# Last image's feed-forward: normalisation as subtraction and product of eight columns, second bias and residual in parts of four columns, and an order of its own

## The chip, the cores and the metric

The kernel runs on one core of one Trainium2 chip. The time is device microseconds (us) of one execution; lower is better. Five engines work side by side, each through a queue of its own in a fixed order: TensorE (PE, its weight loads listed as PEld), VectorE (DVE), ScalarE (ACT), GpSimd (POOL) and SyncE (SP, which only issues transfers here).

## What is computed

The input holds 8 images of 128 × 128 positions with 96 channels, in fp32. One layer is computed. Its first half normalises over the channels, projects to 192 channels, transforms each image with a two-dimensional Fourier transform, multiplies by filters that depend on the image, transforms back, projects to 96 channels and adds the input. Its second half is the feed-forward part, which the change is about:

```python
def _ln_t(v, eps=1e-5):
    m = jnp.mean(v, axis=-1, keepdims=True)
    s = jnp.var(v, axis=-1, keepdims=True)
    return (v - m) / jnp.sqrt(s + eps)
...
def _qlinear(x, W, b):
    y = q_acc(jnp.einsum('bsk,nk->bsn', q_mul(x), q_mul(W)))
    return q_acc(y + q_mul(b))
h = jax.nn.relu(_qlinear(x, W1, b1))
y = _qlinear(h, W2, b2)
...
t = t + _L0_ffn_ref(_ln_t(t), L0_ffn_W1, L0_ffn_b1, L0_ffn_W2, L0_ffn_b2)
```

`q_mul` rounds to a float with 5 exponent and 2 mantissa bits (fp8e5 in the kernel), `q_acc` to one with 5 and 10 (f16). W1 is 384 × 96, W2 is 96 × 384.

## The kernel before

Each image goes through three streams. Stream "a" (function `before`) normalises, projects, squares and makes the first transform, and stores the result in DRAM. Stream "s" (`spectrum`) does the second transform, the filters and the way back, with many small matmuls on quarters of the PE array, and stores to V in DRAM; its last PE step is L1241. Stream "c" (`after`) does the last inverse transform (L1337), the residual and the feed-forward part.

Stream "c" works in 8 blocks of 16 image columns (`WB`); a column is a slice of 96 channels for the 128 rows, one row per partition. A block has 4 quarters of 4 columns (`QW`), so an image has 32 units. For a block: SP loads t, the image's input, and vin from V (L1331, L1332); PE multiplies a quarter of vin (L1337), DVE adds t (L1343) and takes statistics column by column (L793, `measure`). `rstd` then gives the scale and shift of the 16 columns: `variance` on GpSimd (L803 to L807), `root` on ACT (L812), `inverse` on DVE (L816), `rest` on GpSimd (L597 to L600, and L824 to L826 for the shift). `quantise` makes each column t·r + m in fp8e5, on ACT (L1361) or on DVE (L1359); every eighth column is on DVE, and for the last image, number 7, every second.

For a unit, PE transposes 4 columns (`turn`, L1366), a cast brings them to SBUF (`turned`, L1380 on ACT; for image 7 L1378 on DVE), PE makes three products of 128 hidden channels (`first`, L1384), ACT casts each to f16 (L1391), DVE adds the first bias (`biased`, L1395), ACT takes the positive part (L1404; for image 7 the last third on DVE, L1402), PE multiplies with W2 (`second`, L1411) and ACT casts to f16 (`put`, L1422). After the 4 units of a block, GpSimd adds the second bias to the whole block (L1426) and then the block to t (L1429), and SP stores it (L1432). Most tiles have two buffers, t has five.

A planner, `in_order`, fixes the order of each queue before the program is built. Every step is an `Op` with the steps that it needs; the planner plays the five engines with the durations in `COST`, and picks, among the steps that can begin within `WAIT` of the earliest, the one with the lowest place plus `PATIENCE` times its delay (and, on PE, `TURN` for a change between quarter and full array). The place is the window of image and stream in `WINDOWS` plus an offset by kind in `OFFSETS`. `SHARED` names the DVE steps that the planner keeps apart from GpSimd's. Each engine then keeps that order. Streams of different images overlap, so ahead of the last image's end stream "c" of one image lies beside "a" and "s" of later ones. The feed-forward part of image 7 needs the whole stream "s" of image 7 (`load_v` waits for every `store_v`).

`WARM` lists PE steps ahead of which some filler matmuls are issued (`keep_warm`, L587); their output is not used.

Of the kernel before, what the change touches and what calls it, by code (L numbers as in the profile page):

```python
# [68 lines left out]
    "a": ((-1014.7, 224.2), (1155.2, 782.6), (913.1, 640.2), (700.4, 97.1), (81, 727.1), (986.1, 683.8), (1759.7, 398.2), (2087.9, 538.4)),  # L69
    "s": ((159.4, 351.5), (85.6, 1024.7), (720.2, 346.4), (408.4, 331.2), (-141.4, 469.9), (-95.4, 205.3), (797.8, 257), (1809.8, 30.5)),  # L70
    "c": ((1028.7, 511.2), (1109.6, 188.3), (1290.9, 349.7), (1829.7, 439.1), (2176.6, 456.9), (2490.5, 149.5), (2420.5, 484.7), (2163.8, 1143.1)),
}
OFFSETS = {
    "a_context": -69.32,
    "a_fold": 73.44,
    "a_inverse": -262.16,
    "a_load_r": 18.09,
    "a_load_x": 271.95,
    "a_load_xT": -31.56,
    "a_measure": 23.91,  # L80
    "a_project": 117.85,
    "a_put": 26.98,
    "a_rate_e": 26.43,
    "a_rate_n": 275.68,
    "a_rate_p0": -178.47,
    "a_rate_p1": 125.73,
    "a_rate_p2": -434.33,
    "a_rate_v0": -18.7,
    "a_rate_v1": 37.77,
    "a_rate_v2": 27.67,  # L90
    "a_rate_v3": 53.52,
    "a_rectify": -24.16,
    "a_rest": 88.21,
    "a_root": -155.19,
    "a_scale": 83.17,
    "a_square": 92.51,
    "a_store_r": 7.65,
    "a_store_y": -218.91,
    "a_transform": -124.2,
    "a_variance": -11.06,  # L100
    "c_accumulated": -194.42,
    "c_add_up": -37.31,
    "c_bias": -232.6,
    "c_biased": -34.16,
    "c_first": -3.46,
    "c_hidden": -99.06,
    "c_hidden_2": 18.08,
    "c_hidden_v": 120.54,
    "c_inverse": -69.89,
    "c_last": -164.57,  # L110
    "c_load_v": -0.91,
    "c_measure": 206.09,
    "c_put8": 55.17,
    "c_quantise": 161.11,
    "c_quantise_v": 272.29,
    "c_residual": -76.16,
    "c_rest": -195.99,
    "c_root": 122.09,
    "c_second": -129.32,
    "c_store": 584.16,  # L120
    "c_turn8": -377.8,
    "c_turned8": 104.13,
    "c_turned8_v": -71.45,
    "c_variance": -123.83,
    "s_alone_t": 236.02,
    "s_alone_x": 109.24,
    "s_alone_z": 223.71,
    "s_along_w": -28.38,
    "s_combine": -31.52,
    "s_copy_sr": 140.45,  # L130
    "s_filters_of": 27.98,
    "s_invert": 0.86,
    "s_inverted": -111.88,
    "s_load_t": 225.43,
    "s_load_y": 199.13,
    "s_make": 124.58,
    "s_mix": 88.61,
    "s_mix_low": -10.96,
    "s_mixed": -366.14,
    "s_store_v": 136.77,  # L140
    "s_times": -505.74,
    "s_turn_back": 28.39,
    "s_weigh": -53.57,
}
WAIT, PATIENCE, TURN = (0, 0, 0, 0.27, 0.89), (85, 74.3, 16.6, 0.273, 8.9), 454.49
# [5 lines left out]
    ('c', 1): {('second', 12): 4, ('second', 18): 4},  # L151
    ('s', 2): {('along_w', 7): 4},
    ('a', 3): {('project', 6, 0): 3},
    ('c', 5): {('second', 21): 20, ('second', 29): 10},
# [47 lines left out]
    "s_alone_x": (POOL, 1.01, 0),  # L202
    "c_last": (PE, 0.845, 0),
    "c_residual": (DVE, 0.552, 0),
    "c_measure": (DVE, 0.738, 0),
    "c_quantise": (ACT, 0.48, 0),
    "c_quantise_v": (DVE, 0.323, 0),
    "c_turn8": (PE, 0.386, 0),
    "c_turned8": (ACT, 0.59, 0),
    "c_turned8_v": (DVE, 0.68, 0),  # L210
    "c_hidden_v": (DVE, 0.6, 0),
    "c_hidden_2": (ACT, 1.06, 0),
    "c_first": (PE, 0.381, 0),
# [1343 lines left out]
```

## Time and profile before

| | us |
|---|---|
| median of 3 runs | 2740.46 (2726.29 to 2744.11) |
| profiled execution, its own time | 2741.53 |
| its span, from first to last instruction | 2739.4 |

| stage (us) | PE busy | DVE busy | ACT busy | POOL busy | PE clock |
|---|---|---|---|---|---|
| 0 to 200 | 168.68 | 117.96 | 78.80 | 58.86 | 0.87 |
| 200 to 600 | 382.47 | 328.66 | 237.49 | 208.62 | 0.99 |
| whole span | 2517.3 | 2280.6 | 2143.5 | 1691.3 | 0.966 |

Busy times are those in which an engine executes at least one instruction; the clock is the share of full speed that was granted to TensorE. A group of the profile, such as "L1395 DVE TENSOR_TENSOR y<-y,b1q", is one line of the kernel on one engine: output and inputs by the program's names, sizes as partitions × elements, the count, the busy time, the mean duration of one in ns, and then the idle time of the engine just ahead of them with what ended it ("<-ACT y L1391"). In a list of waits, "ACT h L1404 <- DVE y L1395: 14.4, 11, 2.8" reads: ACT was idle ahead of L1404 until L1395 on DVE had ended, for 14.4 us in 11 cases, the longest 2.8. In the order in time, a row has its start, its duration, engine, line and names.

### The profile page before, as it was taken

Reading aid. Unit: us, or ns where it says so; the run is one execution under the profiler, and the core shown is the slowest. Engines: PE = TensorE matmul, PEld = TensorE weight load, DVE = VectorE, ACT = ScalarE, POOL = GpSimd, SP = SyncE. Lnnn points to the kernel's source line nnn. Section 1 sums busy time; section 2 is a strip of 40 time slices with the busy share of each in tenths; the row PEclk is TensorE's granted clock in tenths of the full one; section 3 lists DMA queues with packets and bytes.
Section 4 is the critical chain, followed back from the end, with each engine's and each line's share of the span. In section 5 each row is a group of like instructions: output and inputs, shape, how many; then the busy total and the mean of one; then the engine's idle time right before and its main releaser. Section 6 shows DMA issues by size and latency. Waiting matters only on the chain.

```text
span 2739.4 us, 92861 instructions
## 1 busy us (share of the span) xinstructions
PE 2517.3 (92%) x37514; PEld 1803.0 (66%) x37514; DVE 2280.6 (83%) x5485; ACT 2143.5 (78%) x4332; POOL 1691.3 (62%) x2535
## 2 busy tenths in 40 slices
PE   7899999999899999899999999999999998999887
PEld 4557777767667776666776776766667665666444
DVE  5568697888898888978888988888979988889786
ACT  2356666649889798887998788988989888988866
POOL 3235454546576657756777576857766676788444
PEclk8899999999999999999999999999999999999889
DMA  8789899998867987587768988786768666575341
GB/s 227 243 262 302 255 279 291 285 272 276 260 192 244 291 258 204 186 259 240 231 198 258 289 257 260 224 243 199 234 190 250 192 201 187 153 230 157 107 137 46
DMA packets 506110, 621.22 MB, mean 227 GB/s; under 512 B 165197, under 2 KB 440038, under 8 KB 505658
## 3 DMA queue, kind: packets, MB, share of 16 engines
q1 hardware_dynamic: 417618, 464.28, 57.7%
q10 hardware_dynamic: 88064, 151.02, 15.5%
q8 instruction: 295, 4.83, 0.8%
q14 instruction: 133, 1.09, 0.1%
HBM read 407.03 MB, written 208.16 MB: 225 GB/s over the span
## 4 chain that ended last, share of the span: by engine, by line
PE 42%; ACT 17%; DVE 11%; issue 6%; DMA 4%; POOL 3%; ACTq 0%; SPq 0%; POOLq 0%; DVEq 0%
PE px L881 7%; PE py L910 6%; PE pv L1200 5%; ACT y L1391 4%; PE pf L1119 4%; PE pz L1104 4%; PE pg L1241 4%; PE pk L1337 4%; ACT h L1404 3%; ACT z L1361 3%; PE ph L1384 3%; PE po L1411 2%; DMA vin<-Vd 2%; DVE y L1395 2%; DVE t L1148 1%
## 5 line engine op out<-in xcount | busy, mean ns | idle before, releaser
L881 PE MATMUL px<-W1S,zT 97*128 97x240 f32 x2048 | 505.0, 381 | 10.6 <-DVE yst L922 5.5
L881 PEld LDWEIGHTS px<-W1S,zT 97*128 97x128 f32 x2048 | 393.1, 196 | 123.6 <-PE warm L587 10.4
L1089 POOL TENSOR_TENSOR tw<-tb,r 128x384 f32<-128x384 f32 (+1 forms) x264 | 292.1, 1106 | 259.2 <-PE pf L1119 127.6
L910 PE MATMUL py<-X,F 128*128 128x384 f32 x1024 | 435.3, 515 | 17.0 <-DVE t L1343 3.1
L1391 ACT CAST y<-ph 128x512 f16<-128x512 f32 x768 | 417.1, 604 | 25.6 <-PE ph L1384 21.6
L1404 ACT ACTIVATE h<-y 128x1536 fp8e5<-128x1536 f16 (+1 forms) x256 | 371.1, 1450 | 29.2 <-DVE y L1395 26.3
L892 ACT ACTIVATE rl<-px 128x480 f32<-128x480 f32 x512 | 292.7, 579 | 127.5 <-PE px L881 94.1
L1361 ACT ACTIVATE z<-t,ln_m,ln_r 128x96 fp8e5<-128x96 f32 x848 | 361.3, 475 | 9.1 <-POOL ln_m L826 5.6
L1395 DVE TENSOR_TENSOR y<-y,b1q 128x1536 f16<-128x1536 f16 x256 | 321.5, 1256 | 54.2 <-ACT y L1391 52.8
L906 POOL TENSOR_TENSOR sacc<-sacc,rl 128x192 f32<-128x192 f32 x248 | 175.1, 706 | 289.4 <-ACT rl L892 277.3
L1200 PE MATMUL pv<-w2C,xf 64*64 64x96 f32 x9264 | 315.6, 246 | 28.5 <-issue 25.4
L922 DVE TENSOR_TENSOR yst<-py,yb 128x384 f32<-128x384 f32 x512 | 261.7, 546 | 74.0 <-ACT rl L892 24.2
L1200 PEld LDWEIGHTS pv<-w2C,xf 64*64 64x64 f32 x9264 | 273.2, 134 | 62.7 <-issue 45.7
L1142 DVE TENSOR_TENSOR d<-pz,sr 128x390 f32<-128x390 f32 x512 | 265.2, 554 | 42.1 <-ACT sr L1135 41.7
L1148 DVE TENSOR_TENSOR t<-d,pf 128x780 f32<-128x780 f32 x256 | 245.3, 958 | 53.2 <-PE pf L1119 33.2
L1162 POOL TENSOR_TENSOR xf<-t 128x390 f32<-128x390 f32 x256 | 234.5, 916 | 66.6 <-DVE t L1148 57.6
L1119 PE MATMUL pf<-RW,tw 64*128 64x130 f32 x3120 | 252.4, 292 | 20.8 <-DVE t L1153 11.1
L1104 PE MATMUL pz<-F,yt 64*64 64x65 f32 x12480 | 250.0, 223 | 18.6 <-issue 13.2
L1384 PE MATMUL ph<-zT,W1q 96*128 96x512 fp8e5 x768 | 242.1, 387 | 23.3 <-ACT y L1391 6.5
L1426 POOL TENSOR_TENSOR o<-o,b2q 128x1536 f16<-128x1536 f16 x64 | 200.5, 3132 | 94.1 <-ACT o L1422 93.5
L1104 PEld LDWEIGHTS pz<-F,yt 64*64 64x64 f32 x12480 | 217.3, 136 | 61.4 <-issue 26.9
L1119 PEld LDWEIGHTS pf<-RW,tw 64*128 64x128 f32 x3120 | 201.3, 189 | 82.8 <-issue 30.2
(132 smaller groups left out, 5129.7 us busy)
## 6 DMA issues: line engine op xcount, KB each, us to landing
Yd<-yst ACTq DMA_DIRECT2D x256, 384.0 KB
yt<-Yd SPq DMA_DIRECT2D x248, 384.0 KB
xb<-in_xw SPq DMA_DIRECT2D x64, 768.0 KB
zT<-in_xT SPq DMA_DIRECT2D x128, 384.0 KB
rB<-Rd SPq DMA_DIRECT2D x128, 384.0 KB
tb<-T SPq DMA_DIRECT2D x256, 192.0 KB
Vd<-gst ACTq DMA_DIRECT2D x128, 384.0 KB
t<-in_x SPq DMA_DIRECT2D x64, 768.0 KB
```

What stands on the lines that cost most here:

```text
L881: nc.tensor.matmul(px[:, i * (MED + SCTX) : (i + 1) * (MED + SCTX)], lhsT=zTs[(b * NU // 2 + u // 2) % NZT][:, QW * (u % 2) + i0 + i, :], ...
L892: nc.scalar.activation(kept["rl", u][:, i0 : i0 + 2, :].rearrange("h w m -> h (w m)"), kept.pop(("px", u, i0)), AF.Relu)
L910: nc.tensor.matmul(py, lhsT=F1, rhs=kept["X", u][:, i0 : i0 + 2, :].rearrange("h w m -> h (w m)"), start=True, stop=True)
L1089: nc.gpsimd.tensor_tensor(tw[p, :].rearrange("p (q k m) -> p k q m", q=3, k=2), tb[p, :].rearrange(order, k=2, q=3), rates[b][p, :].rearra ...
L1104: nc.tensor.matmul(halves[i][64 * k : 64 * k + 64, c * L : (c + 1) * L], lhsT=kept["yt", g][rows, 2 * cs + k, 64 * q : 64 * q + 64], rhs=F ...
L1119: nc.tensor.matmul(pf[:, s, q * 2 * L : (q + 1) * 2 * L], lhsT=tw[p, 128 * q : 128 * q + 128], rhs=RW[p, :], start=True, stop=True,)
L1200: nc.tensor.matmul(kept["pv", p, r][half, i * C : (i + 1) * C], lhsT=kept["xf", g][rows, k, q, half], rhs=(w2N if k == 1 and h == 1 else w ...
L1361: nc.scalar.activation(z, t, AF.Identity, bias=m, scale=r, saturate=False)
L1384: nc.tensor.matmul(kept["ph", u, n], lhsT=W1q[:, n * 128 : (n + 1) * 128], rhs=kept["zT", u], start=True, stop=True)
L1391: nc.scalar.copy(kept["y", u][:, n, :], kept.pop(("ph", u, n)))
L1395: nc.vector.tensor_tensor(y, y, b1q, ALU.add)
L1404: nc.scalar.activation(h, y, AF.Relu, saturate=False)
```

## The change

For image 7 alone:

- The normalisation is done for 8 columns at once, in two steps. `centre` on GpSimd subtracts the mean from 8 columns of t and writes into vin; `norm` on DVE multiplies them with r into fp8e5. `rstd` makes the mean (and not the shift) right after the variance. The 16 column-wise instructions of a block become 2 and 2.
- The transposed cast is on ACT (`turned8`), as for the other images; L1378 goes.
- The second bias and the sum with t are made unit by unit (`bias_part`, `add_part`). The last block is stored in four parts (`store_part`); the others are stored whole.
- `load_v` waits for the `norm` of two blocks ahead as well, since vin is written and read later than before.

In addition, `OFFSETS` may hold a value of its own for a kind in image 7 (ending `_8`) and in stream "a" of image 0 (ending `_1`; all of these equal those without the ending). `WINDOWS`, `OFFSETS`, `WAIT`, `PATIENCE`, `TURN` and `WARM` have new values for all images; only a few are shown. `SHARED` stays as it is. The filler matmuls are 510 instead of 472, of which 301 instead of 249 belong to stream "c" of image 7.

```diff
--- before.py
+++ after.py
@@ -66,95 +66,140 @@
 WINDOWS = {
...
-    "c": ((1028.7, 511.2), (1109.6, 188.3), (1290.9, 349.7), (1829.7, 439.1), (2176.6, 456.9), (2490.5, 149.5), (2420.5, 484.7), (2163.8, 1143.1)),
...
+    "c": ((1077.8, 438.5), (962.8, 173.4), (1098.5, 307), (1684.2, 504.4), (1984, 366.6), (2465, 69), (2244, 686.2), (2737, 1205.9)),
 }
 OFFSETS = {
...
+    "c_add_part_8": -199.88,
...
+    "c_bias_part_8": 1548.65,
...
+    "c_centre_8": 49.3,
...
+    "c_norm_8": -808.2,
...
+    "c_residual_8": -2157.99,
...
-WAIT, PATIENCE, TURN = (0, 0, 0, 0.27, 0.89), (85, 74.3, 16.6, 0.273, 8.9), 454.49
+WAIT, PATIENCE, TURN = (0, 0, 0, 0.25, 0.91), (3.5, 1.09, 73.9, 2.99, 3.82), 45.03
...
@@ -203,11 +248,12 @@
     "c_last": (PE, 0.845, 0),
     "c_residual": (DVE, 0.552, 0),
     "c_measure": (DVE, 0.738, 0),
+    "c_centre": (POOL, 1.65, 0),
+    "c_norm": (DVE, 0.95, 0),
     "c_quantise": (ACT, 0.48, 0),
     "c_quantise_v": (DVE, 0.323, 0),
     "c_turn8": (PE, 0.386, 0),
     "c_turned8": (ACT, 0.59, 0),
-    "c_turned8_v": (DVE, 0.68, 0),
     "c_hidden_v": (DVE, 0.6, 0),
     "c_hidden_2": (ACT, 1.06, 0),
     "c_first": (PE, 0.381, 0),
@@ -247,6 +293,9 @@
     "s_load_y": (SP, 0.9, 1.25),
     "s_load_t": (SP, 0.65, 0.576),
     "c_load_v": (SP, 2.1, 4.736),
+    "c_bias_part": (POOL, 0.84, 0),
+    "c_add_part": (POOL, 0.82, 0),
+    "c_store_part": (SP, 0.4, 0.48),
     "s_store_v": (ACT, 0.375, 1),
     "c_store": (SP, 0.4, 1.92),
     "_load_raw": (SP, 1.2, 1),
@@ -377,13 +426,19 @@
     return (stream[0] if stream else "") + "_" + name
 
 
+def group_of(op):
+
+    kind = kind_of(op)
+    return kind + "_1" if op.key[0] == ("a", 0) else kind + "_8" if op.key[0] == ("c", B - 1) else kind
+
+
 def place_of(op):
 
     if op.key[0] is None:
         return op.time
     x, b = op.key[0]
     start, length = WINDOWS[x][b]
-    return start + op.time * length + OFFSETS.get(kind_of(op), 0.0)
+    return start + op.time * length + OFFSETS.get(group_of(op), 0.0)
 
 
 SAME = {"alone_z": "make", "alone_t": "times", "alone_x": "turn_back"}
@@ -792,7 +847,7 @@
         for i in range(q * QW, (q + 1) * QW):
             nc.vector.bn_stats(st[:, i, :], xin[:, i, :])
 
-    def rstd(time, step, pool, key, kept, eps, one, users, mean=False):
+    def rstd(time, step, pool, key, kept, eps, one, users, mean=""):
 
 
         def variance(key):
@@ -806,6 +861,10 @@
             nc.gpsimd.tensor_scalar(d, d, C / 4, C * eps, ALU.mult, ALU.add)
             nc.gpsimd.tensor_tensor(v, v, d, ALU.add)
             kept["vd", key] = v, d
+            if mean == "centre":
+                m = kept["m", key] = pools[pool].tile([128, WB], F32, name="ln_m", tag="ln_m")
+                nc.gpsimd.tensor_tensor(m, st[:, :, 1], st[:, :, 4], ALU.add)
+                nc.gpsimd.tensor_scalar(m, m, 0.5, None, ALU.mult)
 
         def root(key):
             r = pools[pool].tile([128, WB], F32, name="ln_r", tag="ln_r")
@@ -819,14 +878,15 @@
             v, d = kept.pop(("vd", key))
             r, st = kept["r", key], kept.pop(("st", key))
             newton(r, v, d, C)
-            if mean:
+            if mean == "shift":
                 m = pools[pool].tile([128, WB], F32, name="ln_m", tag="ln_m")
                 nc.gpsimd.tensor_tensor(m, st[:, :, 1], st[:, :, 4], ALU.add)
                 nc.gpsimd.tensor_tensor(m, m, r, ALU.mult)
                 nc.gpsimd.tensor_scalar(m, m, -0.5, None, ALU.mult)
                 kept["m", key] = m
 
-        at(time, variance, key, after=[one("measure", key, q) for q in range(NQ)] + [one("rest", key - 2)])
+        free = [one("centre", key - 2, h) for h in range(2)] if mean == "centre" else []
+        at(time, variance, key, after=[one("measure", key, q) for q in range(NQ)] + [one("rest", key - 2)] + free)
         at(time + step, root, key, after=[one("variance", key)] + users)
         at(time + 1.5 * step, inverse, key, after=[one("root", key)])
         at(time + 2 * step, rest, key, after=[one("inverse", key)])
@@ -1319,7 +1379,7 @@
     def after(b, t0, P):
 
         stream[0] = "c", b
-        blocks = ("measure", "variance", "rest", "load_v", "store", "add_up", "turn8", "residual", "last", "quantise", "quantise_v")
+        blocks = ("measure", "variance", "rest", "load_v", "store", "add_up", "turn8", "residual", "last", "quantise", "quantise_v", "norm", "centre")
         one = named("c", b, {None: NU, **dict.fromkeys(blocks, NWB)})
         kept = {}
 
@@ -1348,7 +1408,19 @@
             add_stats(kept["st", blk], kept["t", blk], q)
 
         def quantiser(i):
-            return "quantise_v" if i % 8 == 7 or b == B - 1 and i % 2 == 1 else "quantise"
+            return "norm" if b == B - 1 else "quantise_v" if i % 8 == 7 else "quantise"
+
+        def centre(blk, h):
+            w = slice(h * HB, (h + 1) * HB)
+            m = kept["m", blk][:, w].unsqueeze(2).to_broadcast([128, HB, C])
+            nc.gpsimd.tensor_tensor(kept["vin", blk][:, w, :], kept["t", blk][:, w, :], m, ALU.subtract)
+
+        def norm(blk, h):
+            if ("z8", blk) not in kept:
+                kept["z8", blk] = pools["c"].tile([128, WB, C], F8, name="z8", tag="z8")
+            w = slice(h * HB, (h + 1) * HB)
+            r = kept["r", blk][:, w].unsqueeze(2).to_broadcast([128, HB, C])
+            nc.vector.tensor_tensor(kept["z8", blk][:, w, :], kept["vin", blk][:, w, :], r, ALU.mult, saturate=False)
 
         def quantise(blk, i):
             if ("z8", blk) not in kept:
@@ -1374,10 +1446,7 @@
         def turned(u):
             kept["zT", u] = pools["c"].tile([C, QW * 128], F8, name="zT8", tag="zT8")
             pz = kept.pop(("pz",) + divmod(u, NQ))[:C, :]
-            if b == B - 1:
-                nc.vector.tensor_copy(kept["zT", u], pz, saturate=False)
-            else:
-                nc.scalar.activation(kept["zT", u], pz, AF.Copy, saturate=False)
+            nc.scalar.activation(kept["zT", u], pz, AF.Copy, saturate=False)
 
         def first(u, n):
             kept["ph", u, n] = bank("ph")
@@ -1428,6 +1497,18 @@
         def add_up(blk):
             nc.gpsimd.tensor_tensor(kept["t", blk], kept["t", blk], kept["o", blk], ALU.add)
 
+        def bias_part(blk, q):
+            o = kept["o", blk][:, q * QW : (q + 1) * QW, :]
+            nc.gpsimd.tensor_tensor(o, o, b2q.unsqueeze(1).to_broadcast([128, QW, C]), ALU.add)
+
+        def add_part(blk, q):
+            w = slice(q * QW, (q + 1) * QW)
+            nc.gpsimd.tensor_tensor(kept["t", blk][:, w, :], kept["t", blk][:, w, :], kept["o", blk][:, w, :], ALU.add)
+
+        def store_part(blk, q):
+            w0 = blk * WB + q * QW
+            nc.sync.dma_start(out=out[b, :, w0 : w0 + QW, :], in_=kept["t", blk][:, q * QW : (q + 1) * QW, :])
+
         def store(blk):
             nc.sync.dma_start(out=out[b, :, blk * WB : (blk + 1) * WB, :], in_=kept.pop(("t", blk)))
 
@@ -1438,25 +1519,31 @@
             t = t0 + u * P
             blk, q = divmod(u, NQ)
             if q == 0:
-                after = [one("last", blk - 2, n) for n in range(NQ)] + [one("store", blk - 5)]
+                after = [one("last", blk - 2, n) for n in range(NQ)] + [one("norm", blk - 2, h) for h in range(2)] + [one("store", blk - 5)]
                 after += [(("s", b), "store_v", p) for p in range(NP)]
                 if b == 0 and blk < 2:
                     after += [(None, "next_pool")]
                 at(t - 0.004, load_v, blk, after=after)
-                users = [one(k, blk - 2, i) for i in range(WB) for k in ("quantise", "quantise_v")]
-                rstd(t, 0.3 * P, "c", blk, kept, 1e-5, one, users, mean=True)
+                users = [one(k, blk - 2, i) for i in range(WB) for k in ("quantise", "quantise_v", "norm")]
+                rstd(t, 0.3 * P, "c", blk, kept, 1e-5, one, users, mean="centre" if b == B - 1 else "shift")
             at(t, last, blk, q, after=[one("load_v", blk)], banks=1, until=[one("residual", blk, q)])
             at(t + 0.0003, residual, blk, q, after=[one("last", blk, q)])
             at(t, measure, blk, q, after=[one("residual", blk, q), one("rest", blk - 2)])
-            for i in range(QW):
+            if b == B - 1 and q % 2:
+                h = q // 2
+                after = [one("residual", blk, n) for n in (q - 1, q)] + [one("last", blk, n) for n in (q - 1, q)]
+                at(t, centre, blk, h, after=[one("variance", blk)] + after)
+                after = [one("rest", blk), one("centre", blk, h)] + [one("turn8", blk - 2, n) for n in range(NQ)]
+                at(t, norm, blk, h, after=after)
+            for i in range(QW if b < B - 1 else 0):
                 at(
                     t + 0.2 * i * P, quantise, blk, q * QW + i,
                     name=quantiser(q * QW + i),
                     after=[one("rest", blk), one("residual", blk, q)] + [one("turn8", blk - 2, n) for n in range(NQ)],
                 )
-            after = [one(quantiser(q * QW + i), blk, q * QW + i) for i in range(QW)]
+            after = [one("norm", blk, q // 2)] if b == B - 1 else [one(quantiser(q * QW + i), blk, q * QW + i) for i in range(QW)]
             after += [one("first", u - 2, n) for n in range(NHC)]
-            turned8 = "turned8_v" if b == B - 1 else "turned8"
+            turned8 = "turned8"
             at(t, turn, blk, q, name="turn8", after=after, banks=1, until=[one(turned8, u)])
             after = [one("turn8", blk, q)] + [one("first", u - 2, n) for n in range(NHC)]
             at(t + 0.0003, turned, u, name=turned8, after=after)
@@ -1471,13 +1558,21 @@
             for name, *part in hiddens:
                 at(t, hidden, u, *part, name=name, after=[one("biased", u), one("second", u - 2)])
             at(
-                t, second, u, after=[one(name, u, *part) for name, *part in hiddens] + [one("add_up", blk - 2)],
+                t, second, u, after=[one(name, u, *part) for name, *part in hiddens] + [one("add_up", blk - 2)] + [one("add_part", blk - 2, n) for n in range(NQ)],
                 banks=1, until=[one("put8", blk, q)],
             )
-            at(t + 0.0003, put, blk, q, name="put8", after=[one("second", u), one("add_up", blk - 2)])
-            if q == NQ - 1:
+            at(t + 0.0003, put, blk, q, name="put8", after=[one("second", u), one("add_up", blk - 2)] + [one("add_part", blk - 2, n) for n in range(NQ)])
+            if b == B - 1:
+                at(t, bias_part, blk, q, after=[one("put8", blk, q)])
+                zs = [one("centre", blk, q // 2)]
+                at(t, add_part, blk, q, after=[one("bias_part", blk, q)] + zs)
+                if blk == NWB - 1:
+                    at(t, store_part, blk, q, after=[one("add_part", blk, q)])
+                elif q == NQ - 1:
+                    at(t, store, blk, after=[one("add_part", blk, n) for n in range(NQ)])
+            elif q == NQ - 1:
                 at(t, bias, blk, after=[one("put8", blk, n) for n in range(NQ)])
-                zs = [one(quantiser(i), blk, i) for i in range(WB)]
+                zs = [one(k, blk, i) for i in range(WB) for k in ("quantise", "quantise_v", "centre")]
                 at(t, add_up, blk, after=[one("bias", blk)] + zs)
                 at(t, store, blk, after=[one("add_up", blk)])
 
```

## The prediction

> **What bounds the kernel now.** I read the 40 slices first, then sums by stage, then groups, waits and order in time for the last stage. TensorE leads: 2517.3 of 2739.4 us busy, 92% of the span. The sums by stage (us; each engine's busy time with its count; granted clock, DMA share, GB/s) show that this doesn't hold to the end:
>
> ```profile
> 600.00:2534.00 1934.00, 1802.16 (x30604) 1325.22 (x30604) 1682.41 (x3854) 1680.90 (x3460) 1332.74 (x1863) 0.98 0.75 228
> 2534.00:2739.40 205.40, 163.98 (x1071) 87.79 (x1069) 151.53 (x336) 146.32 (x284) 91.04 (x118) 0.90 0.31 97
> ```
>
> The columns are PE, its weight loads, DVE, ACT, POOL. Up to 2534 us PE is busy 93% of the time. From 2534 us on, when the last spectral product (L1241) is done, only the feed-forward of images 6 and 7 is left. I call this the tail. No engine fills it: PE 80%, DVE 74%, ACT 71%, POOL 44%, and the groups of the tail show that 70.6 us of PE's 164 are filler (L587):
>
> ```profile
> L587 PE MATMUL warm<-zeros 128*64 128x512 bf16 x279 | 70.6, 400 | 1.0 <-DVE zT L1378 0.9
> ...
> L1395 DVE TENSOR_TENSOR y<-y,b1q 128x1536 f16<-128x1536 f16 x38 | 47.4, 1251 | 22.8 <-ACT y L1391 22.4
> ...
> L1359 DVE TENSOR_SCALAR z<-t,ln_r,ln_m 128x96 fp8e5<-128x96 f32 x66 | 35.0, 565 | 1.1 <-POOL ln_m L826 1.1
> ...
> L1361 ACT ACTIVATE z<-t,ln_m,ln_r 128x96 fp8e5<-128x96 f32 x79 | 31.9, 478 | 2.1 <-POOL ln_m L826 2.1
> ...
> L1378 DVE CAST zT<-pz 96x512 fp8e5<-96x512 f32 x32 | 21.8, 682 | 10.2 <-PE pz L1366 9.7
> ```
>
> The mean of z on DVE, 565 ns, is far above its median over the run (322 ns), and y's 1251 above its 959. The order in time says why; two such places, DVE and then POOL:
>
> ```profile
> 2674.85 2.96 DVE L1359 TENSOR_SCALAR z<-t,ln_r,ln_m 128x96 fp8e5<-128x96 f32 x1
> ...
> 2678.60 3.09 DVE L1359 TENSOR_SCALAR z<-t,ln_r,ln_m 128x96 fp8e5<-128x96 f32 x1
> ...
> 2674.66 3.08 POOL L1426 TENSOR_TENSOR o<-o,b2q 128x1536 f16<-128x1536 f16 x1 [16.33 <-ACT o L1422]
> 2677.82 3.80 POOL L1429 TENSOR_TENSOR t<-t,o 128x1536 f32<-128x1536 f32 x1
> ```
>
> A 0.3 us instruction lasts as long as the block-wide GpSimd addition beside it. Against their shortest forms I count 32 us of such excess on y, z and h in the tail, 13 of 14 cases between 1.0 and 2.9 us. Last, what ACT and POOL wait for in the tail:
>
> ```profile
> POOL o L1426 <- ACT o L1422: 70.2, 8, 16.3
> ...
> ACT h L1404 <- DVE y L1395: 14.4, 11, 2.8
> ...
> ACT o L1422 <- PE po L1411: 10.1, 10, 2.8
> ACT ln_r L812 <- POOL ln_v L807: 9.9, 3, 4.7
> ...
> ACT y L1391 <- PE ph L1384: 8.5, 8, 3.3
> ```
>
> So the tail is a loop PE, ACT, DVE, PE in which each waits for the others, with GpSimd cutting in. ACT idles 59 us of 205: the 43 above, 4 on smaller rows, 10.5 at the end, after its last instruction.
>
> **What the Trainium skill says.** "SBUF — State Buffer", section "Who interferes with whom": DVE in a two-port mode, or with two inputs in SBUF, and GpSimd exclude each other for a whole instruction. The trace agrees (2.96 beside 3.08 us). The new product reads two SBUF tiles (vin, ln_r), so by this page it too is blocked by GpSimd, though the planner's set SHARED leaves it out. "VectorE: DVE Perf Modes", section "Why `tensor_tensor` can't do 2×_2P or 4×": fp32 stays at one element per cycle, so 768 columns at 0.96 GHz are 0.80 us at least (an estimate from the page). The nearest row, L1148 with 780 columns and one PSUM input, has a median of 957 ns.
>
> **The change part by part** (image 7: 8 blocks of 16 columns, 32 units of 4).
>
> 1. *Normalisation.* 128 instructions go: 64 on DVE (0.24 us each in a row: 15 us, without stalls) and 64 on ACT (0.36 us each in a row: 23). In come 16 products on DVE at 0.80 to 0.96, I take 0.9: 14 us; and 16 subtractions on GpSimd. GpSimd's two-input additions cost 0.888 us at 390 columns and 3.1 at 1536, on a line 1.62 at 768: 26 us. The mean's statistics change by one instruction of 0.25 per block: nothing. The 32 transposed casts move from DVE (0.60 in a row, 19 us off) to ACT (0.49, 16 us on). Net: DVE −20, ACT −7, GpSimd +26.
> 2. *Bias and residual in parts.* 16 instructions become 64 at 0.88: 50 us become 56. The longest hold of the shared port falls from 3.1 us to 0.9, or 1.6 for a subtraction. y (42 in the new tail), h (32) and the products (16) then meet shorter waits, oftener: 90 of them at 0.6 (chance that GpSimd is busy: about 120 of 185 us) × 0.45 (half a hold) are 24 us, against 32. More important is what waits behind: ACT's 14.4 us for y drop to 5, I estimate, since y can no longer be held up by 3 us; the square root's 9.9 us behind whole-block additions to 5. Both estimates could be zero gains.
> 3. *The end.* The last bias and sum, 3.08 + 3.09 us, become 0.88 + 0.88: −4.4. The last store is a quarter as large; from the end of the sum at 2735.2 to the span's end are 4.2 us, of which 0 to 3 may go, I take 1.5. Together −6, on the path for certain.
> 4. *Waits added.* In the built order GpSimd does variance, mean, both subtractions, and only then the rest of the rstd: 3.2 us are put ahead of it, and product and transpose wait for it; square root and reciprocal cover about 1.5. Eight times 1.7 are 14 us if nothing hides it; blocks run in pairs, with units of the earlier pair between, so I take +3. Behind a subtraction that waits for its residual stand the parts of bias and sum of earlier blocks, for which only stores and the L1422 casts two blocks on wait: nothing. The buffer vin is freed by the product instead of the last L1337, so loads of V start some us later; the load at 2639.2 feeds products up to 2649.6, and there are two buffers: taken as nothing, at most 8 × 2 us. SP issues the same loads and three more small stores; loads now stand in pairs behind pairs of stores, and the same cover hides it.
> 5. *Order.* The planner's constants and windows are new for all images, so every queue is reshuffled. The built orders nevertheless look alike: 566 and 572 switches between quarter-array and full matmuls on PE, the same sequence of stages. After the last L1241 stand 41 units instead of 39: two units of image 6 move into the tail. They cost ACT there about 3.7 us each (three casts 1.43, h 1.37, zT 0.49, o 0.37) and save about as much ahead: nothing. Filler matmuls ahead of the last L1241 fall from 176 to 134; 42 × 0.25 are 10 us of PE where PE bounds, half of it in true gaps: −5. Otherwise the reshuffle ahead of 2534 us is unknown: PE idles 150 us between 200 and 2534, and a tenth either way is ±15, taken as 0.
>
> The sum, on ACT as the engine that carries the tail (about 146 us of work before and after: −7 and the +7 of the two units): idle for y −9, for the square root −5, the end −6, idle behind PE −2 (PE waited for z and zT on DVE), work −7, subtraction ahead of rstd +3, filler −5: −31. Rounding against myself by 2 for PE, which carries more filler (see below): −29 from the profiled 2741.5, **2712 us**. That execution lies 1 us above the median of the runs, 2740.46, and within their spread of 18.
>
> **Rivals.**
>
> *A. The filler becomes the work.* The new tail has 376 filler matmuls instead of 296. PE busy 164 + 80 × 0.25 + 4.5 for two units are 188 us, at the mean clock of 0.90; with about 10 us of unavoidable idle the tail is 198 instead of 205 + 7: −14, less what a full clock gives back. With the −5 ahead: 2722. For it: filler was on the chain with 3.6 us at 2614. Against it: filler stands where PE waits.
>
> *B. The shared port decides, and it ends slower.* GpSimd in the tail: 56 + 26 + statistics 20 + three whole pairs of image 6 19 = 121 us; y 42 × 0.88, h 32 × 0.33, products 14, together 62. If they exclude each other fully, 183 us, against 84 + 60 = 144 before, which filled 70% of 205. If again only 75% can be filled, the tail is 244 instead of 212: +32, less 6 and 5: 2763, 23 above the median; the worst additions under 4 would pass 1%. It decides once usable filling stays below about 84%. Against it: the small GpSimd instructions overlap their start with a DVE hold, and shorter holds pack better.
>
> *C. The reshuffle ahead dominates.* ±15 us there on top of any case; for 2712 it gives 2697 to 2727.
>
> *D. Nothing changes in the tail*, because latency through buffers of two sets the pace, not work: only the end's −6 and −5 remain: 2730.
>
> **How the numbers follow.** Forecast with its reshuffle, somewhat better or worse: 0.58; A 0.12; D 0.12; B 0.18. A measurement of this kernel tells about 1% from no change: below 2713 or above 2768. Of the forecast's share some five sevenths fall below 2713, since both unknown stalls and packing could give more than I booked; from the others 0.08. That gives faster 0.50. B puts 0.15 past 2768, with its added waits and C's loss; a little more comes from C alone: slower 0.17. Same: 0.33. The range leaves one in ten out on either side: low 2675 (forecast; the rest of the gaps for y and the root gone, −10; stalls at the port halved, −12; C −15), high 2755 (most of B).
>
> **What would show it.** Right: DVE busy in the tail near 125 us, ACT near 146, no y, z or h above 2.7 us except beside image 6's additions; the last GpSimd addition near 0.9 us; 35 or so idle us on ACT. Products well over 1 us mean the port blocks them. A tail over 205 us with GpSimd and port-bound DVE work near 183 is B; PE over 95% with filler is A; a tail shorter by 25 with the same end is C. The forecast is wrong if the tail shrinks by less than 10 us, or if the stretch ahead moves by more than 15.

## The result, and the profile after

| | before | changed |
|---|---|---|
| median of 15 runs each (us) | 2738.36 (2723.9 to 2748.74) | 2716.31 (2709.7 to 2732.18) |
| span of the profiled execution (us) | 2739.4 | 2712.0 |
| granted TensorE clock in it | 0.966 | 0.976 |

The ratio is 0.9929, interval 0.9908 to 0.995. That is 19 us of 2738 (14 to 25), where 29 were forecast; the two medians lie 22 us apart.

The tail begins when the last spectral product has ended: at 2526.6 us before and at 2514.6 us after. I cut both profiles there (the prediction took 2534 for it before, 7 us late). The columns of the sums by stage are again PE, its weight loads, DVE, ACT and POOL, then clock, DMA share and GB/s. Before:

```profile
2526.60:2739.40 212.80, 170.50 (x1111) 90.94 (x1110) 156.98 (x339) 153.72 (x300) 98.03 (x125) 0.90 0.32 101
```

After:

```profile
600.00:2514.60 1914.60, 1780.27 (x30647) 1317.04 (x30648) 1676.13 (x3861) 1661.10 (x3430) 1333.03 (x1849) 0.98 0.75 230
2514.60:2712.00 197.40, 177.37 (x1240) 95.93 (x1238) 143.13 (x268) 155.01 (x286) 155.30 (x193) 0.98 0.36 115
```

The tail has become 15.4 us shorter. ACT works as long in it as before (153.7 and 155.0 us), so its idle time carries all of the difference: 59.1 us before, 42.4 after. GpSimd has gone from 98 to 155 us, and DVE has lost only 14. The other 12 us of the two spans lie ahead of the tail. The experiments show below that this point moves by more than that between executions, so I don't count them as an effect.

The groups of the tail after, to be read against those of L1395, L1359 and L1378 before (same columns):

```profile
L1464 DVE TENSOR_TENSOR y<-y,b1q 128x1536 f16<-128x1536 f16 x42 | 53.9, 1283 | 29.4 <-ACT y L1460 29.4
L1506 POOL TENSOR_TENSOR t<-t,o 128x384 f32<-128x384 f32 x32 | 39.8, 1242 | 2.5
...
L1502 POOL TENSOR_TENSOR o<-o,b2q 128x384 f16<-128x384 f16 x32 | 36.1, 1128 | 8.7 <-ACT o L1491 8.7
...
L1423 DVE TENSOR_TENSOR z<-vin,ln_r 128x768 fp8e5<-128x768 f32 x16 | 30.6, 1948 | 1.5 <-POOL ln_r L655 1.4
...
L1416 POOL TENSOR_TENSOR vin<-t,ln_m 128x768 f32<-128x768 f32 x16 | 24.1, 1524 | 0.7
L1471 DVE TENSOR_SCALAR h<-y 128x512 fp8e5<-128x512 f16 x32 | 23.5, 735 | 1.5
```

The product takes 1.95 us on average, twice its shortest form of 0.97. Bias and sum in parts take 1.13 and 1.24, where they take 0.91 at the very end, when DVE is silent. So both engines lengthen each other. The worst place is in the order in time, DVE first:

```profile
2566.76 7.60 DVE L1423 TENSOR_TENSOR z<-vin,ln_r 128x768 fp8e5<-128x768 f32 x2
2574.28 0.41 DVE L1471 TENSOR_SCALAR h<-y 128x512 fp8e5<-128x512 f16 x1
```

The same stretch on POOL, which works there on a block of image 6 (still whole additions):

```profile
2566.70 3.08 POOL L1495 TENSOR_TENSOR o<-o,b2q 128x1536 f16<-128x1536 f16 x1 [2.50 <-ACT o L1491]
2569.86 3.68 POOL L1498 TENSOR_TENSOR t<-t,o 128x1536 f32<-128x1536 f32 x1
```

Two products last 7.60 us. The two additions beside them (3.08 and 3.68) end at 2573.54, 0.8 us before the products do. Behind the products stands an h on DVE, and for that h ACT waits, as PE and ACT show:

```profile
2570.12 0.82 PE L1453 MATMUL ph<-zT,W1q 96*128 96x512 fp8e5 x3
2574.81 1.56 ACT L1460 CAST y<-ph 128x512 f16<-128x512 f32 x3 [6.26 <-DVE h L1471]
```

PE has made the products for the next y by 2570.94. But y has two buffers, and ACT's cast (`accumulated`) may fill one only when the h of two units earlier has been made from it (`old_hidden`); that h ends at 2574.69. This is the single case of 6.3 us in what ACT waits for in the tail after:

```profile
ACT y L1460 <- PE ph L1453: 7.9, 8, 1.6
...
ACT o L1491 <- PE po L1480: 6.7, 6, 2.7
ACT y L1460 <- DVE h L1471: 6.3, 1, 6.3
...
ACT h L1473 <- DVE y L1464: 6.0, 6, 1.8
...
ACT ln_r L871 <- POOL ln_v L862: 1.0, 1, 1.0
```

The first row answers to y behind ph before (8.5 us); h behind y has fallen from 14.4 to 6.0 us, and the square root behind the variance from 9.9 to 1.0. The wait of 6.3 us is new. Last, the end on POOL after:

```profile
2706.28 0.91 POOL L1506 TENSOR_TENSOR t<-t,o 128x384 f32<-128x384 f32 x1
2707.15 0.91 POOL L1502 TENSOR_TENSOR o<-o,b2q 128x384 f16<-128x384 f16 x1
2708.13 0.91 POOL L1506 TENSOR_TENSOR t<-t,o 128x384 f32<-128x384 f32 x1
```

ACT's last cast, after and then before:

```profile
2706.57 0.48 ACT L1491 CAST o<-po 128x384 f16<-128x384 f32 x1 [1.80 <-PE po L1480]
```

```profile
2728.37 0.48 ACT L1422 CAST o<-po 128x384 f16<-128x384 f32 x1 [0.78 <-PE po L1411]
```

It ends at 2707.05, and the span 4.95 us later; before, at 2728.85 and 10.55 us later.

### The profile page after: what moved, and what is told of

It reads as the page before. It is cut to its first block, busy times and chain, and to the rows that moved or that the text cites. A ratio compares the mean times of both kernels' runs of the same rounds, so it can differ in the third digit from the quotient of the medians.

```text
span 2712.0 us, 92856 instructions
## 1 busy us (share of the span) xinstructions
PE 2503.9 (92%) x37552; PEld 1796.8 (66%) x37552; DVE 2258.1 (83%) x5405; ACT 2126.5 (78%) x4300; POOL 1746.2 (64%) x2591
## 3 DMA queue, kind: packets, MB, share of 16 engines
q10 hardware_dynamic: 88064, 151.02, 15.4%
## 4 chain that ended last, share of the span: by engine, by line
PE 56%; ACT 17%; DMA 9%; DVE 9%; issue 5%; POOL 3%; SPq 1%; ACTq 0%; POOLq 0%; DVEq 0%
PE px L941 11%; PE py L970 9%; PE pv L1260 7%; PE pf L1179 5%; PE pz L1164 5%; PE pg L1301 5%; ACT y L1460 4%; PE pk L1397 4%; ACT h L1473 4%; DMA vin<-Vd 3%; PE ph L1453 3%; PE po L1480 3%; ACT z L1433 2%; DMA zT<-in_xT 2%; PE warm L642 2%
## 5 line engine op out<-in xcount | busy, mean ns | idle before, releaser
L941 PE MATMUL px<-W1S,zT 97*128 97x240 f32 x2048 | 495.7, 377 | 10.1 <-DVE yst L982 5.3
L941 PEld LDWEIGHTS px<-W1S,zT 97*128 97x128 f32 x2048 | 387.9, 194 | 119.4 <-DVE yst L982 10.5
L1464 DVE TENSOR_TENSOR y<-y,b1q 128x1536 f16<-128x1536 f16 x256 | 306.5, 1197 | 79.5 <-ACT y L1460 78.6
L1433 ACT ACTIVATE z<-t,ln_m,ln_r 128x96 fp8e5<-128x96 f32 x784 | 337.1, 479 | 6.7 <-POOL ln_m L885 3.6
L966 POOL TENSOR_TENSOR sacc<-sacc,rl 128x192 f32<-128x192 f32 x248 | 168.9, 681 | 259.1 <-ACT rl L952 240.5
L970 PEld LDWEIGHTS py<-X,F 128*128 128x128 f32 x1024 | 183.7, 194 | 95.7 <-issue 20.4
```

The source lines that it names most:

```text
L941: nc.tensor.matmul(px[:, i * (MED + SCTX) : (i + 1) * (MED + SCTX)], lhsT=zTs[(b * NU // 2 + u // 2) % NZT][:, QW * (u % 2) + i0 + i, :], ...
L970: nc.tensor.matmul(py, lhsT=F1, rhs=kept["X", u][:, i0 : i0 + 2, :].rearrange("h w m -> h (w m)"), start=True, stop=True)
L1433: nc.scalar.activation(z, t, AF.Identity, bias=m, scale=r, saturate=False)
L1464: nc.vector.tensor_tensor(y, y, b1q, ALU.add)
```

## The experiments

Each ratio is against the kernel before, run on the same chip. For each profile I give the tail, from its own last spectral product to the end of the span. It is that of one execution, which can lie well off the median of its kernel (`centre_dve`: 2717.93 us profiled, 2732.81 in the median). Most kernels have the code of the change with two lists, `NORM` and `PARTS`, that name the images with the new normalisation and with additions in parts:

```diff
+NORM, PARTS = (B - 1,), (B - 1,)
...
-            return "norm" if b == B - 1 else "quantise_v" if i % 8 == 7 else "quantise"
+            return "norm" if b in NORM else "quantise_v" if i % 8 == 7 or b == B - 1 and i % 2 == 1 else "quantise"
...
-            if b == B - 1:
+            if b in PARTS:
                 at(t, bias_part, blk, q, after=[one("put8", blk, q)])
```

### Where the gain sits: the order ahead or the last image

`old_front_new_tail` has all order constants of the kernel before, and for image 7 alone the new instructions, offsets, window and filler. Up to image 7's feed-forward its queues are those of the kernel before.

```diff
 WINDOWS = {
...
-    "c": (..., (2420.5, 484.7), (2163.8, 1143.1)),
+    "c": (..., (2420.5, 484.7), (2737, 1205.9)),
...
 WAIT, PATIENCE, TURN = (0, 0, 0, 0.27, 0.89), (85, 74.3, 16.6, 0.273, 8.9), 454.49
```

> The new instructions and offsets for image 7, with the old tables for everything else: every queue is that of the kernel before until the last image's feed-forward starts. Theory (the tail gains by its own instructions): most of the gain stays, 2738 - 16 = about 2722 us, ratio to the kernel before 0.994. Rival (the reshuffle ahead brings the gain): 2736 us, ratio 0.999 to 1.000.

`new_front_old_tail` is the opposite: the new constants for all but image 7, and there the old instructions, offsets, window and filler.

```diff
-    "c": (..., (2244, 686.2), (2737, 1205.9)),
+    "c": (..., (2244, 686.2), (2163.8, 1143.1)),
...
+NORM, PARTS = (), ()
```

> The new tables for everything but image 7's feed-forward, which has its old instructions, offsets, window and filler. Theory: 2738 - 6 = about 2732 us, ratio 0.998. Rival (reshuffle): about 2720 us, ratio 0.993. If the two kernels' gains don't add up to the whole 22 us, front and tail depend on each other.

Measured: `old_front_new_tail` 2711.26 us, ratio 0.9924 (0.9906 to 0.9941), tail 191.9 us. `new_front_old_tail` 2781.27 us, 1.0172 (1.0147 to 1.0197), tail 257.1 us. The first one settles the question: with the old order ahead the whole gain is there, somewhat more than was expected. The second is slower than both of its expectations. It can't be read as a sum, since the choices of the planner's order (`PATIENCE`) are common to all images, and the old offsets and filler counts of image 7 meet another order: its tail is 44 us longer than the one they were made for.

### One part undone, the rest left alone

`undo_parts` has the new normalisation, but whole-block additions for image 7.

```diff
-NORM, PARTS = (B - 1,), (B - 1,)
+NORM, PARTS = (B - 1,), ()
```

> The changed kernel with second bias, residual and store by whole blocks again in image 7 (the normalisation stays new). Theory: the end's 6 us return, and y and h wait up to 3 us behind GpSimd: 2716 + 6 + 8 = 2730 us. Rival (pace set by latency through pairs of buffers): only the end returns, 2722 us.

`undo_norm` has the parts, but the normalisation by column and the transposed casts on DVE.

```diff
-NORM, PARTS = (B - 1,), (B - 1,)
+NORM, PARTS = (), (B - 1,)
```

> The changed kernel with image 7's normalisation by single columns on ACT and DVE again and the transposed cast on DVE (the parts stay). Theory: DVE has 20 us more and ACT 7 more: 2716 + 8 = 2724 us. Rival (the shared port decides: the new products last 1.95 us each in the mean and GpSimd carries 24 us of subtractions, so the normalisation gives nothing or costs): 2716 or below, down to 2708 us.

Measured: `undo_parts` 2736.3 us, 1.0004 (0.9985 to 1.0024), tail 221.2 us. `undo_norm` 2766.02 us, 1.0117 (1.0091 to 1.0143), tail 242.3 us. `undo_parts` lies 6 us above its theory, `undo_norm` 42 above. Taken at their word, the normalisation would be worth 51 us, more than the whole change. The chain of `undo_norm` in its tail makes one suspicious (shares by line, then three of its pieces: start, duration, count):

```profile
by line: PE warm L647 21.4%; issue 15.3%; ACT h L1481 8.2%; ACT y L1468 7.3%; POOL o L1510 6.8%; PE pk L1402 5.8%; PE po L1488 5.7%; ACT z L1438 5.0%; POOL t L1514 4.9%; PE ph L1461 3.7%; DVE st L853 2.0%; ACT o L1499 1.9%; DVE zT L1455 1.8
...
2575.59 5.73 PE warm L647 x17
...
2642.01 4.48 PE warm L647 x20
...
2680.05 4.29 PE warm L647 x15
```

A fifth of 203 us is filler, up to 5.7 us at a time. The counts were set for an order in which PE waits at those places; in another order the filler itself may be what is waited for. The same can be said of the offsets. So neither run prices its part yet.

### The filler

`no_filler` is the changed kernel without image 7's 301 filler matmuls, in the same order.

```diff
 WARM = {
...
-    ('c', 7): {('last', 0, 0): 3, ('first', 2, 0): 17, ('first', 3, 0): 17,
...
 }
```

> The changed kernel without the 301 filler matmuls of image 7's feed-forward (all else in the same order on every engine). Theory: filler stands mostly in gaps and holds the clock up: without it 2716 to 2726 us, with a lower granted clock in the tail than 0.98. Rival A (filler is the work that sets the end): 10 us or more faster, 2706 us or below.

Measured: 2719.03 us, 0.992 (0.9895 to 0.9946). The line of its tail:

```profile
2515.40:2709.50 194.10, 134.00 (x939) 77.94 (x937) 143.40 (x268) 155.30 (x286) 157.43 (x193) 0.76 0.37 116
```

PE is busy 43 us less and its granted clock falls from 0.98 to 0.76, yet DVE, ACT and the length hardly move. The kernel's own matmuls even take longer (`first`: 378 ns in the mean with filler, 470 without). In the order it was set for, the filler neither sets the end nor helps, as far as 9 us either way can be told. The chain of the changed kernel shows how easily one is misled here:

```profile
by line: PE warm L642 15.8%; DVE z L1423 10.0%; POOL t L1506 8.2%; POOL o L1502 7.6%; ACT y L1460 6.9%; ACT h L1473 6.2%; issue 6.1%; PE po L1480 4.9%; PE ph L1453 4.3%; DVE y L1464 4.0%; ACT z L1433 3.6%; PE pk L1397 3.2%; POOL vin L1416 3
```

15.8% of 197 us are 31 us of filler on the chain, and taking it away gains nothing that can be measured. In its place PE now waits: 33.2 us for h on ACT ahead of `second`, where the changed kernel has 2.5.

### The change carried further

`parts_67` makes the additions in parts for image 6 as well, whose whole additions hold the products in the trace; `parts_all` for all images.

```diff
-NORM, PARTS = (B - 1,), (B - 1,)
+NORM, PARTS = (B - 1,), (B - 2, B - 1)
```

> The changed kernel with bias and residual in parts of four columns for image 6 too. Theory (holds of the shared port by whole blocks delay DVE): the two pairs of products that take 7.6 us each behind whole-block additions of image 6 shrink to some 3.3 us; 5 to 9 us of DVE delay go, 2711 us. Rival (products have slack): unchanged, 2714 to 2718 us.

> Bias and residual in parts of four columns for all images. Theory: ahead of the tail PE bounds and DVE's waits behind GpSimd are covered, while 8 x 48 more instructions on GpSimd cost 6 us per image there without effect; order ahead changes, so 2700 to 2725 us. Rival (port holds limit the whole kernel): 20 us or more faster, 2695 us or below.

`centre_dve` moves the subtraction from GpSimd to DVE.

```diff
-            nc.gpsimd.tensor_tensor(kept["vin", blk][:, w, :], kept["t", blk][:, w, :], m, ALU.subtract)
+            nc.vector.tensor_tensor(kept["vin", blk][:, w, :], kept["t", blk][:, w, :], m, ALU.subtract)
...
-    "c_centre": (POOL, 1.65, 0),
+    "c_centre": (DVE, 0.95, 0),
```

> The changed kernel with the 16 subtractions on DVE instead of GpSimd. Theory: DVE gains 16 x 0.9 = 14 us of work and GpSimd loses 24: about even, 2714 to 2722 us. Rival B (the shared port limits the tail): faster by 5 us or more, 2711 us or below, since GpSimd's 155 us in the tail shrink to about 130.

Measured: `parts_67` 2736.81 us, 1.0002 (0.9984 to 1.002), tail 224.4; `parts_all` 2747.15 us, 1.0038 (1.002 to 1.0056); `centre_dve` 2732.81 us, 0.9977 (0.9959 to 0.9995), tail 216.5. All three lose the gain or most of it, and none of the expectations held. They too have another order than the filler was set for, so the first was repeated without it (below). The other two were not, and what they would be worth in an order of their own stays open.

### The parts priced without filler and in an order of their own

In four more kernels image 7 has no filler (in `parts_67_2` image 6 neither), so that they compare with `no_filler`. In three of them the `_8` offsets and the length of image 7's window are chosen anew, so that the kernel's own plan ends as early as it can for these instructions.

```diff
 OFFSETS = {
...
-    "c_first_8": -1055.54,
+    "c_first_8": -881.56,
...
-NORM, PARTS = (B - 1,), (B - 1,)
+NORM, PARTS = (), (B - 1,)
```

That is `undo_norm_2`; `undo_parts_2` (`PARTS = ()`) and `parts_67_2` (`PARTS = (B - 2, B - 1)`) are edited alike. `undo_order_2` keeps the changed instructions and takes image 7's own offsets away:

```diff
-    "c_first_8": -1055.54,
...
+    "c_norm": 163.76,
+    "c_centre": -211.52,
+    "c_bias_part": -208.64,
+    "c_add_part": -72,
```

> Image 7's normalisation by single columns on ACT and DVE again, as in undo_norm, but without the 301 filler matmuls of image 7 (they had been counted out for the gaps of another order) and with image 7's offsets chosen anew by the planner's rule. Theory (work and waits of the tail decide): 2719 + 8 = about 2727 us; what undo_norm lost beyond that was misplaced filler. Rival (the new normalisation itself brings most): 2745 us or more. Second rival (the port eats the new normalisation's gain): 2720 us or below.

> Second bias, residual and store by whole blocks again in image 7, as in undo_parts, without image 7's filler and with its offsets chosen anew. Theory: the end's 6 us and some 6 of waiting behind GpSimd return: 2719 + 12 = 2731 us. Rival (only the end counts): 2725 us. Second rival (the loss of undo_parts was filler in the wrong place): 2721 us or below.

> The changed kernel's instructions without offsets of its own for image 7 (each kind takes the value of the other images; subtraction, product and parts those of the nearest old kind), and without image 7's filler. Theory (the new instructions carry the gain): 2719 to 2729 us. Rival (the order set apart for image 7 carries it): 2735 us or more.

> Parts of four columns for images 6 and 7, as in parts_67, without the filler of both and with image 7's offsets chosen anew. Theory (parts_67 lost by filler counted out for another order, and its shorter holds do help): 2708 to 2716 us. Rival (more and smaller GpSimd instructions beside the end of stream s cost more than they give): 2730 us or more.

| | median (us) | ratio | tail (us) | ACT busy | ACT idle |
|---|---|---|---|---|---|
| `no_filler` | 2719.03 | 0.992 (0.9895 to 0.9946) | 194.1 | 155.3 | 38.8 |
| `undo_norm_2` | 2717.26 | 0.9927 (0.9901 to 0.9953) | 193.1 | 161.1 | 32.0 |
| `undo_parts_2` | 2733.04 | 0.9981 (0.9964 to 0.9998) | 210.8 | 155.8 | 55.0 |
| `undo_order_2` | 2725.03 | 0.9958 (0.994 to 0.9976) | 206.5 | 157.1 | 49.4 |
| `parts_67_2` | 2725.91 | 0.9958 (0.994 to 0.9976) | 210.8 | 163.5 | 47.3 |

Differences below are between ratios, their intervals added in squares, times 2737 us. One reserve holds for the three with offsets chosen anew: a better choice may exist for them, so what they say a part is worth may be too much, not too little. And all four lean on the six runs of `no_filler`, three at 2710 to 2714 us and three at 2724 to 2727.

**The normalisation is worth nothing that can be measured**: 0.0007 ± 0.0037 against `no_filler`, 2 ± 10 us. The tail of `undo_norm_2` says why:

```profile
2522.70:2715.80 193.10, 132.85 (x940) 77.55 (x937) 147.40 (x348) 161.08 (x318) 122.60 (x185) 0.80 0.37 117
```

With the old normalisation DVE works 147.4 us instead of 143.4 and ACT 161.1 instead of 155.3, while GpSimd works 35 us less. On DVE the 16 products (31.2 us in `no_filler`) save some 11 us against the z and zT that they replace (21.9, of which four are image 6's, and 21.8), but y beside the busier GpSimd takes 55.5 us instead of 48.8. What ACT gains in work it pays back as idle time. Of the 52 us between `undo_norm` and `undo_norm_2` I can't say which share is the filler and which the offsets.

**The parts are worth 17 ± 8 us** (0.0061 ± 0.0031). Two of the waits in the tail of `undo_parts_2`:

```profile
PEld L1309 <- DVE z L1294: 35.6, 8, 6.6
...
ACT zT L1323 <- PE pz L1309: 20.4, 8, 3.4
```

L1294 is the product there. One such place, DVE and then POOL, which works on a whole addition of image 7:

```profile
2626.11 3.84 DVE L1294 TENSOR_TENSOR z<-vin,ln_r 128x768 fp8e5<-128x768 f32 x1
```

```profile
2625.45 3.68 POOL L1372 TENSOR_TENSOR t<-t,o 128x1536 f32<-128x1536 f32 x1
```

The transpose on PE waits 4.5 us in the mean for the product, eight times, and ACT behind it idles 20.4 us, where `no_filler` has 1.1 us in that row. The end is 10.5 us after the last cast, as before the change, where `no_filler` has 6.5. So ACT's idle time is 16 us longer: 19 by this wait and 4 by the end, less some 7 on the other rows.

**The order of its own is worth 10 ± 9 us** (0.0038 ± 0.0031); the interval only just excludes nothing. Three waits of `undo_order_2`:

```profile
PEld L1358 <- ACT h L1351: 59.7, 33, 3.4
...
ACT o L1369 <- PE po L1358: 23.2, 23, 2.8
...
ACT zT L1327 <- PE pz L1313: 10.3, 7, 5.3
```

The product takes only 1.31 us there, so the port is less of a burden than in the changed kernel; but ACT runs into the product po 23 times (7 times and 7.0 us in `no_filler`) and waits 10.3 us for the transposes (1.1). PE waits for h on ACT in both kernels alike (59.7 us here, 52.3 in `no_filler`), so the difference lies in ACT's waiting for PE. Against the changed kernel with its filler (0.9929) the difference is 8 ± 8 us: that the order is worth something is likely, and no more can be said.

**Parts for image 6** do shorten the worst products (2.21 us at most instead of 3.85), and the time is still 10 ± 9 us longer than that of `no_filler`: ACT has 8 us more of work in the tail (127 casts of y are left to do there, where `no_filler` has 123), and 8.5 us more of idle time, most of it behind po (22.4 us against 7.0). So shortening the products that were held for 7.6 us did not shorten the kernel; whether it would in another order stays open. No kernel here is measurably faster than the changed one: `old_front_new_tail` lies within its interval.

**What was not run** is the kernel before with an order for image 7 chosen anew, that is old normalisation and whole additions without filler. How much such an order alone would bring, and whether the parts would be worth 17 us without the new product, stays open.

### How still the part ahead stands

The time of the last spectral product's start, in one profile each of kernels whose queues are the same up to image 7's feed-forward: 2499.1 in `centre_dve`, 2507.1 in `undo_parts`, 2514.1 changed, 2514.9 in `no_filler`, 2522.2 in `undo_norm_2`, 2528.6 in `undo_parts_2`. With the order ahead of the kernel before: 2526.2 and 2523.8. A difference of 12 us there between two single profiles is no evidence.

## Why the prediction was right, and where it wasn't

The direction and the place were right: the gain lies in the tail, in ACT's idle time and in the end. ACT's idle time fell by 16.7 us, where the terms for it (−9, −5, −6, −2, +3) make −19. 19 us of 29 came in all. That the sum is so near is in part luck: the normalisation is worth nothing where −7 of work was booked for it, the order probably something where nothing was, and the parts came near their −20 (−9, −5 and −6) by another wait than those named.

- *The end, −6*: 5.6 us measured (10.55 to 4.95). Right.
- *Work on ACT, 0 with two more units*: 153.7 and 155.0 us. Right; `undo_norm_2` has 5.8 us more than `no_filler`, where −7 was booked.
- *Square root behind additions, 9.9 to 5*: 1.0 us. Better by 4. The parts don't explain it: with whole additions this wait is gone in `undo_parts_2`, with parts it is 3.5 us in `no_filler` and 6.9 in `undo_norm_2`. It follows the order.
- *ACT's wait for y, 14.4 to 5*: 6.0 us as such, but 6.3 us came back as one wait for h and its buffer, h being queued behind the two long products. Step 2 said that nothing could be held up by 3 us any more, and yet image 6's whole additions lie beside image 7's first products. The net is about −2, the largest miss of the sum.
- *Waits added, +3* (step 4): next to nothing. The products wait 1.4 us for r in the whole tail, and no transpose waits for a product.
- *Idle behind PE, −2*: 10.1 + 8.5 us before, 6.7 + 7.9 and, for the transposed casts now on ACT, 1.9 after. −2, right.
- *Normalisation, DVE −20 and GpSimd +26 (step 1), stalls at the port 32 to 24 (step 2)*: the term that failed. The prediction priced the product at 0.9 us and gave every port-bound instruction the same stall, 0.6 × 0.45 = 0.27 us, 24 us for 90 of them. Reckoned from the shortest forms of this tail (y 0.93, product 0.97, h 0.40), the stalls are 42 × 0.35 + 16 × 0.98 + 32 × 0.34, about 41 us: y and h came near the booked size, the product met nearly four times that. So DVE was busy 143 us, not 125. The product's price was also low by itself: its shortest form, 0.97 us, lies above the whole range considered, 0.80 to 0.96. GpSimd's subtractions were priced about rightly (24 us for 26), but the 64 parts took 76 us instead of 56 and the statistics 37 instead of 20, so GpSimd took 155 instead of 121. `undo_norm_2` confirms the consequence: the new normalisation brings nothing. The Trainium skill's "SBUF — State Buffer", section "Who interferes with whom", on which the step rested, agrees with the place shown (7.60 us beside 3.08 + 3.68); it was the product's exposure that I set too low.
- *Filler ahead, −5*: nothing can be seen. *The reshuffle ahead, 0 ± 15*: right as 0; `old_front_new_tail` has the full gain without it.
- *The order of image 7's own offsets*: booked at nothing, without a reason. `undo_order_2` gives it 10 us, with the doubt of its interval.
- *The parts*: booked with −6 at the end and with the shorter waits of y (−9) and root (−5). They brought 17 together, most of it through a wait that the prediction didn't name: the transpose behind a product behind a whole addition. As the product belongs to the new normalisation, the parts may in the first place pay for what it brings; no run separates the two.

Of the rivals, A (the filler becomes the work) falls with `no_filler`. B (the shared port decides) had the mechanism right: it ate the normalisation's gain on DVE. Its sum of work was right too. Reckoned from the shortest form of each instruction in the trace, GpSimd has 123 us in the tail and y, products and h on DVE 66, together 189, where B has 183. The two sides are in progress at the same time for 94 us, but 77 of these are the lengthening of one or the other; by this estimate only some 17 us of work ran side by side. What B had wrong is the packing: it allowed three quarters of the tail to be filled, and 189 of 197 us were, so the kernel didn't become slower. C falls with `old_front_new_tail`. D (only the end) falls with `undo_parts_2`: there is more to the parts than 5.6 us. The test "the stretch ahead moves by no more than 15" was met with 12 us, but single profiles can't carry it.

## What to carry to other kernels

Before work with two inputs in SBUF is moved to DVE beside a busy GpSimd, price it at its own time plus the holds that it will meet, not at its time alone; and when GpSimd must work there, try cutting its instructions short, since what waits is not the blocked instruction alone but the chain behind it. That was worth 17 ± 8 us in image 7, and nothing in image 6 in the orders tried. Filler matmuls and order constants belong to one order: an experiment that changes the order must drop or re-choose them, or it measures them. A share of the chain is not a price: 31 us of filler on it were worth nothing that could be measured, so take the thing away and measure. And a wait that ends with a DVE instruction may be one for a buffer, as ACT's 6.3 us were: PE had finished its product 3.9 us earlier.

## What the hardware showed that I had not expected

The holds work both ways, and on small instructions as well: GpSimd's 384-column sum takes 0.91 us beside a silent DVE and 1.24 on average in the tail. And TensorE's clock had no say in the tail that these runs can show: at 0.98 and at 0.76 granted, the medians are 2716.31 and 2719.03 us, with ratios to the kernel before that can't be told apart (0.9929 and 0.992).
